# k's and q's features in one VectorE operation, inverse sums in PSUM, and the output pair's second half moved, in a two-block attention kernel

## The chip, the cores and the metric

The kernel runs on one NeuronCore of a Trainium2 chip. A core has five engines that run their own instruction queues in order and wait for each other through semaphores: TensorE (PE, matrix products), VectorE (DVE), ScalarE (ACT), GpSimd (POOL) and SyncE (SP, which only issues transfers here). Each has access to SBUF, the main on-chip memory; TensorE writes its results to PSUM, which has eight banks of 128 partitions x 512 fp32 values, and VectorE and ScalarE read them from there. The metric is the time of one execution on the device in microseconds (us). The kernel before takes 3023.89 us, the median of three runs (3023.61 to 3024.01).

## The reference

The input x is (8, 512, 64, 64): 8 images, 512 channels, 4096 positions. Two blocks follow each other, all in fp32.

The first block is softmax attention whose keys and values are max-pooled two by two, with 64 channels for f and g and 256 for v:

```python
f = conv1x1(x, Wf, bf).reshape(b, c // K, h * w)
g = maxpool2x2(conv1x1(x, Wg, bg))      # 1024 keys
v = maxpool2x2(conv1x1(x, Wh, bh))
s = jnp.einsum('bcn,bcm->bnm', f, g)
beta = jax.nn.softmax(s, axis=-1)
o = jnp.einsum('bcm,bnm->bcn', v, beta).reshape(b, c // 2, h, w)
x = gamma * conv1x1(o, Wv, bv) + x
```

The second is linear attention with 64 features for q and k:

```python
def delu(x):
    return PARAM * jax.nn.relu(x) + jnp.exp(PARAM * jnp.minimum(x, 0.0))   # PARAM = 10
Qf = delu(Q).transpose(0, 2, 1)
Kf = delu(K)
KV = jnp.einsum('bmn,bcn->bmc', Kf, V)
norm = 1.0 / jnp.einsum('bnd,bd->bn', Qf, jnp.sum(Kf, axis=-1) + EPS)
attn = jnp.einsum('bnd,bdc,bn->bcn', Qf, KV, norm)
out = x + gamma[0] * attn
```

KV and the sum of Kf need all positions of an image, so an image's second block can be finished only when its last position has been through the first.

## The kernel before, in words

An image is cut into 8 chunks of 512 positions, 64 chunks in all. The kernel is one software pipeline over steps s (function `step`); chunk s goes through the main part in step s. In the same step the projections of chunk s + 9 are made, so that pooled g and v of a whole image are ready before its first chunk is attended, and the image before is finished (`c_here`). Each step records its work as pairs of a number and a function, `at(t, fn, ...)`, sorts them by the number, and calls them in that order. The numbers are places in an order, not times that anything waits for. The engines PE, DVE, ACT and POOL keep the order written; only semaphores, and buffers that must come free, hold an instruction up.

In step s the work on TensorE stands in this order:

- M1 (line L433), the transposes of k of chunk s - 1 (`turn_k`, tile pkT, L581), M2, and the product of k and x of chunk s - 1 (`gather`, pg, L593), in even steps of an image to be finished pd (`normalize`, L673), then M3;
- the scores of chunk s + 1 (`weigh`, s, L347) between M6, M5, M7 and M4. M1 to M7 are the seven products of a Strassen-Winograd scheme for v times E (`attend`), E being the exponentials of the scores;
- in odd steps the first half of an output pair (`finish`, pa, L700): four matmuls of 512 columns from k's and v's product and q. A pair is two chunks whose q features share one tile (qq): one in the upper 64 partitions, the other in the lower;
- f and g of chunk s + 9 (`a_fg`, fg, L232), and tot (L390), the sums of E of chunk s + 1 over the keys, as a product with ones;
- N1 to N7 (`project`, L490), the output projection of chunk s as a Winograd scheme, H1 to H7 (`a_h`, L276), the projection to v of chunk s + 9;
- in odd steps the second half of the pair (pa again), the transposes of the pooled v (`a_turn`, pvT), k and q of chunk s (`features`, pk, L547), the transposes of x of chunk s (`turn_x`, px, L574). Then the next step's M1.

VectorE, in the same step: sums for M's outputs and E's sums r (L383, L386); the pooling of g (L209); `invert` (L395), the reciprocals of tot into an SBUF tile rtot; the N outputs (L506 to L523); `normalize_block` (L409), four multiplications of E of chunk s + 1 by rtot, with the H outputs (L285 to L299) in between; the pooling of v (vp, L209); the block sum T1 of E (`sums_of_e`, L415); the features kk (L560) and qq (L564), min(exp, 1) + relu, each for its half of the partitions; then T2, T3, T4 (L418 to L424). kk keeps k of one chunk in one half of the partitions and zeros in the other; its accumulator output goes to ks, from which `start_kb` (L616 to L623) sums k at the start of the next image and writes kb, the matrix of pd.

ScalarE makes the exponentials, copies from PSUM (m1, n1, h1, y, xT, kT), f's halves, x's bias, and `look` (L399, L400), which sums tot and its reciprocals into chk. After the pipeline chk is tested, and only if a sum was too large or small the whole is run again in another form. GpSimd makes some sums of E, the H inputs (tha, thb), adds the N outputs onto x (`residual`, L500), and issues the transfers that add y to the output in memory (L706). SyncE issues loads and the stores of x.

All PSUM tiles come from one pool of eight banks. A new tile takes a bank that is free in the written order, and its first matmul waits for the last reader of the tile that had the bank before. The pools named in the diff (f, q, y and others) work likewise in SBUF.

Of the kernel before, what the change touches and what calls it, by code (L numbers as in the profile page):

```python
# [42 lines left out]
P = 128  # L43
# [5 lines left out]
def tile_two_attention_blocks(  # L49
# [75 lines left out]
    nc.gpsimd.memset(ones, 1.0)  # L125

    kk = const.tile([P, CH], F32, name="kk")
    nc.gpsimd.memset(kk, 0.0)

    kb = const.tile([P, P], F32, name="kb")  # L130
    nc.gpsimd.memset(kb, 0.0)
# [29 lines left out]
    def half(e):  # L161
        return slice(e * D, (e + 1) * D)

    def run(ctx, general):
        xa = ctx.enter_context(tc.tile_pool(name="xa", bufs=2))
        xb = ctx.enter_context(tc.tile_pool(name="xb", bufs=2))
        yc = ctx.enter_context(tc.tile_pool(name="yc", bufs=1))
        image = ctx.enter_context(tc.tile_pool(name="image", bufs=2))
        fpool = ctx.enter_context(tc.tile_pool(name="fpool", bufs=10))
        qpool = ctx.enter_context(tc.tile_pool(name="qpool", bufs=6))  # L170
        work1 = ctx.enter_context(tc.tile_pool(name="work1", bufs=1))
        work = ctx.enter_context(tc.tile_pool(name="work", bufs=2))
        temp = ctx.enter_context(tc.tile_pool(name="temp", bufs=7))
# [41 lines left out]
        def image_of(a):  # L215
            b, j = divmod(a, NCHUNK)
            if j == 0 and b not in st:
                st[b] = {
                    "g": image.tile([P, MT // 2, P], F32, tag="g", name=f"g_{b}"),
                    "vT": image.tile([P, MT, CV], F32, tag="vT", name=f"vT_{b}"),  # L220
                    "ks": image.tile([P, NCHUNK // 2], F32, tag="ks", name=f"ks_{b}"),
                    "G": image.tile([P, C], F32, tag="G", name=f"G_{b}"),
                }
            return st[b]
# [166 lines left out]

        def invert(s):

            rtots[s] = work1.tile([P, CH], F32, tag="rtot", name=f"rtot_{s}")
            nc.vector.reciprocal(rtots[s], totals[s])  # L395

        def look(s):
# [75 lines left out]
        def project(s, at, t):  # L473

            m = {}

            def bias():
                for k in range(KT):
                    xs = x_b[s][:, k, :]
                    nc.scalar.activation(xs, xs, AF.Identity, bias=gb_v0[:, k : k + 1])  # L480

            def product(i):
                o, u = os_[s], to[s]
                b = {
                    1: o[:, 0, 0:HN], 2: o[:, 1, 0:HN], 3: o[:, 1, HN:CH],
                    4: u[:, 3], 5: u[:, 0], 6: u[:, 1], 7: u[:, 2],
                }[i]
                m[i] = bank(f"N{i}_{s}").rearrange("p (k n) -> p k n", k=2)
                for k in range(2):
                    nc.tensor.matmul(m[i][:, k, :], w_v7[i][:, bass.ts(k, P)], b, start=True, stop=True)  # L490
                if i == 1:
                    m["n1"] = part("n1")
                    nc.scalar.copy(m["n1"], m[1])

            def part(name):
                return scratch(f"{name}_{s}").rearrange("p (k n) -> p k n", k=2)

            def residual(i, j, u):
                d = x_b[s][:, 2 * i : 2 * i + 2, bass.ts(j, HN)]
                nc.gpsimd.tensor_tensor(d, d, u, ALU.add)  # L500

            def out(i):
                tt = nc.vector.tensor_tensor
                if i == 2:
                    u = part("n2")
                    tt(u, m["n1"], m[2], ALU.add)  # L506
                    residual(0, 0, u)
                elif i == 6:
                    m["u2"] = part("w2")
                    tt(m["u2"], m["n1"], m[6], ALU.add)  # L510
                elif i == 5:
                    u = part("n3")
                    tt(u, m["u2"], m[5], ALU.add)  # L513
                    tt(u, u, m[3], ALU.add)  # L514
                    residual(0, 1, u)
                elif i == 7:
                    m["u3"] = part("w3")
                    tt(m["u3"], m["u2"], m[7], ALU.add)
                    tt(m["u2"], m["u3"], m[5], ALU.add)
                    residual(1, 1, m["u2"])  # L520
                else:
                    u = part("n4")
                    tt(u, m["u3"], m[4], ALU.subtract)  # L523
                    residual(1, 0, u)

            def store():
                b, j = divmod(s, NCHUNK)
                nc.sync.dma_start(out=outr[b, :, :, bass.ts(j, CH)], in_=x_b[s])

            at(t - 7.4, bias)  # L530
            for n, i in enumerate((1, 2, 3, 6, 5, 7, 4)):
                at(t + 0.86 * n, product, i)
            for i, d in ((2, 3.4), (6, 4.1), (5, 4.8), (7, 6.2), (4, 7.6)):
                at(t + d, out, i)
            at(t + 10.0, store)

        def features(s, at, t):

            b, j = divmod(s, NCHUNK)
            e = j % 2  # L540
            k, q = half(e), half(1 - e)
            m = {}

            def product():
                pk = bank(f"pk_{s}")
                for i in range(KT):
                    nc.tensor.matmul(  # L547
                        pk, w_kqk[:, i, e * D : (e + 2) * D], x_b[s][:, i, :],
                        start=(i == 0), stop=(i == KT - 1),
                    )  # L550
                ex, r = m["ex"], m["r"] = scratch(f"e_{s}"), scratch(f"r_{s}")

                nc.scalar.activation(ex, pk, AF.Exp, bias=b10_kq[:, e : e + 1], scale=PARAM)
                nc.scalar.activation(r, pk, AF.Relu, bias=b10_kq[:, e : e + 1], scale=PARAM)

            def out():
                if e == 0:
                    qq[s // 2] = qpool.tile([P, CH], F32, tag="qq", name=f"qq_{s // 2}")
                ex, r = m["ex"], m["r"]
                nc.vector.scalar_tensor_tensor(  # L560
                    kk[k, :], ex[k, :], 1.0, r[k, :], ALU.min, ALU.add,
                    accum_out=st[b]["ks"][k, j // 2 : j // 2 + 1],
                )
                nc.vector.scalar_tensor_tensor(  # L564
                    qq[s // 2][q, :], ex[q, :], 1.0, r[q, :], ALU.min, ALU.add
                )

            at(t, product)
            at(t + 4.9, out)

        def turn_x(s, t):
            px = bank(f"px_{s}_{t}")
# [39 lines left out]
        def start_kb(b):  # L612

            s = st[b]
            kp = small.tile([P, 1], F32, tag="kp", name=f"kp_{b}")
            nc.vector.tensor_reduce(kp, s["ks"], AX.X, ALU.add)  # L616
            kx = small.tile([P, 1], F32, tag="kx", name=f"kx_{b}")
            nc.vector.tensor_copy(kx[0:D], kp[D : 2 * D])
            nc.vector.tensor_copy(kx[D : 2 * D], kp[0:D])
            ksum = s["ksum"] = image.tile([P, 1], F32, tag="ksum", name=f"ksum_{b}")  # L620
            nc.vector.tensor_tensor(ksum, kp, kx, ALU.add)
            for e in range(2):
                nc.vector.tensor_scalar(  # L623
                    kb[half(e), half(e)], ones[half(e), 0:D], ksum[half(e)], EPS, ALU.mult, ALU.add
                )
# [57 lines left out]
        def finish(pair, ks, at, t):  # L683
# [4 lines left out]
            def product():  # L688
                kv = st[b]["kv"]

                last = b == B - 1 and (2 * pair + ks[0] // 2) % 3 > 0
                pool_ = xa if last else yc
                y = m["y"] = pool_.tile(
                    [P, 2, 2, CH], F32, tag="xa" if last else "y", name=f"y_{pair}_{ks[0]}"
# [22 lines left out]
        def step(s):  # L717
# [24 lines left out]
                at(1.7, turn_k, s - 1)  # L742
                gather(s - 1, at, 3.9)
            if c_here and j == 0:
                at(1.8, start_kb, b_c)
                turn_G(b_c, at, 18.2 if here else 6.0)
                make_KV(b_c, at, 36.5 if here else 8.2)
            if c_here and here and j % 2 == 0:
                normalize(pair, at, 5.79)
            if c_here and not here and j == 0:  # L750
# [1 line left out]
                    normalize(pair + i, at, t)  # L752
            if c_here and j % 2 == 1:
                finish(pair, (0, 1), at, 18.2)
                finish(pair, (2, 3), at, 36.5)
            if 0 <= a < TOTAL:
                a_h(a, at, 20.7, 30.5, 40.8)
                a_fg(a, at, 20.0)
            if 0 <= a - 1 < TOTAL:
                at(5.0, bias_v, a - 1)  # L760
                at(38.3, a_turn, a - 1)
                if a % NCHUNK == 0:
                    at(39.0, sums_of_v, (a - 1) // NCHUNK)
            if after:
# [7 lines left out]
                at(15.9, lambda: add_next(n, nc.vector, "r1", es[n][:, 6, :]))  # L772
                at(17.3, lambda: add_next(n, nc.vector, "r1", es[n][:, 7, :]))
                at(18.1, lambda: add_next(n, nc.vector, "r1", sums[n, "r0"]))
                at(23.4, total, n)
                at(24.5, invert, n)
                if not general:
                    at(27.9, look, n)
                at(32.6, normalize_block, n, 0, 1)
                at(34.2, normalize_block, n, 0, 0)  # L780
                at(38.4, normalize_block, n, 1, 1)
                at(39.6, normalize_block, n, 1, 0)
                at(42.2, sums_of_e, n, 1)
            if here:
                project(s, at, 24.4)
                features(s, at, 38.6)
                for t in range(NT):
                    at(42.1 + t * 0.45, turn_x, s, t)
# [61 lines left out]
```

## Time and profile before

| | us | share of the span | instructions |
|---|---|---|---|
| span of the profiled execution | 3028.2 | | 32619 |
| PE, matmuls | 2871.4 | 95% | 11936 |
| DVE | 2411.3 | 80% | 3102 |
| ACT | 1110.7 | 37% | 2249 |
| POOL | 1132.2 | 37% | 809 |
| L409, E times rtot, 256 of them | 410.6 | | 1629 ns each |
| L395, the reciprocals of tot, 64 | 214.9 | | 3358 ns each |
| L560 and L564, kk and qq, 64 each | 49.5 and 48.7 | | 773 and 761 ns each |
| L703, copies of the output pair to y, 256 | 133.4 | | 600 ns each |

PE's time is that of matmuls; loads of weights (PEld) overlap them. A matmul record [...] may overlap the next: eight records of fg are 3.60 us in the timeline where each has a mean of 603 ns. The granted TensorE clock is a share of full speed, 0.982 in the mean over this run. In a list of waits each line gives the engine with the tile and line that waited, the one it waited for, and then microseconds in total, how often, and the longest. In a timeline a line gives start, duration, engine, line, operation, tiles and form, and in brackets the idle time of the engine ahead of it and who ended it.

The steps before 134 us fill the pipeline, those from 2957 us on empty it; from about 2620 us on there is no chunk s + 9 any more, so fg and H are gone.

### The profile page before, as it was taken

How to read it: one execution, taken by the hardware profiler on the slowest of the kernel's cores; microseconds unless marked ns; L12 is line 12 of the kernel's file. 1: busy time of each engine (PE TensorE's matmuls, PEld its weight loads, DVE VectorE, ACT ScalarE, POOL GpSimd, SP SyncE). 2: the span in 40 equal slices, each digit the busy share in tenths (PEclk: the TensorE clock that was granted, in tenths of full speed). 3: DMA queues.
4: the chain of work that ended last, by engine and by line, in shares of the span. 5: the costliest groups of instructions: out<-in, count | busy, mean ns of one | idle time of the engine just before them, and what ended most of it. 6: DMA issues, size and time to landing. Idle time of an engine off the chain costs nothing.

```text
span 3028.2 us, 32619 instructions
## 1 busy us (share of the span) xinstructions
PE 2871.4 (95%) x11936; PEld 1923.3 (64%) x11936; DVE 2411.3 (80%) x3102; ACT 1110.7 (37%) x2249; POOL 1132.2 (37%) x809
## 2 busy tenths in 40 slices
PE   8999999999999999999999999999999999999994
PEld 5666666666666666666666666666666666656662
DVE  4778878878788778888788788888788888788872
ACT  2333333333333333333433434333333433434432
POOL 4532434433443434333344333434325334232231
PEclk9999999999999999999999999999999999999997
DMA  5122212334234233333243333342233342233337
GB/s 179 51 75 84 70 56 84 98 84 111 75 93 112 74 108 91 91 98 111 70 121 89 82 99 99 97 111 84 74 108 96 99 112 56 70 98 84 84 84 154
DMA packets 128328, 280.98 MB, mean 93 GB/s; under 512 B 8480, under 2 KB 8992, under 8 KB 128160
## 3 DMA queue, kind: packets, MB, share of 16 engines
q1 hardware_dynamic: 105600, 209.73, 20.1%
q0 software_dynamic: 17408, 67.11, 12.6%
q10 hardware_dynamic: 5152, 1.97, 0.3%
q8 instruction: 97, 1.59, 0.2%
q14 instruction: 71, 0.58, 0.1%
HBM read 144.58 MB, written 134.22 MB: 92 GB/s over the span
## 4 chain that ended last, share of the span: by engine, by line
PE 55%; DVE 30%; issue 10%; ACT 3%; POOL 1%; DMA 0%; DVEq 0%; POOLq 0%; ACTq 0%
PE M L433 25%; DVE E L409 10%; PE s L347 8%; PE fg L232 7%; PE pg L593 4%; ACT f L250 3%; PE pa L700 2%; PE pk L547 2%; PE H L276 2%; DVE T L415 1%; DVE vp L209 1%; DVE n L513 1%; DVE n L514 1%; DVE n L506 1%; PE px L574 1%
## 5 line engine op out<-in xcount | busy, mean ns | idle before, releaser
L500 POOL TENSOR_TENSOR xb<-xb,n 128x512 f32<-128x512 f32 x192 | 306.2, 1595 | 560.7 <-DVE n L506 506.3
L351 ACT ACTIVATE E<-s 128x512 f32<-128x512 f32 x512 | 264.1, 603 | 634.0 <-PE s L347 628.7
L383 POOL TENSOR_TENSOR r<-E 128x512 f32<-128x512 f32 x64 | 81.0, 1266 | 983.0 <-ACT E L351 983.0
L409 DVE TENSOR_TENSOR E<-E,rtot 128x1024 f32<-128x1024 f32 x256 | 410.6, 1629 | 0.0
L433 PE MATMUL M<-T,S 128*128 128x256 f32 x1536 | 365.4, 388 | 0.0
L433 PEld LDWEIGHTS M<-T,S 128*128 128x128 f32 x1536 | 281.4, 190 | 128.7 <-ACT E L351 47.8
L433 PE MATMUL M<-E,vT 128*128 128x256 f32 x1024 | 268.3, 409 | 3.5 <-DVE E L409 3.5
L347 PE MATMUL s<-f,g 64*128 64x512 f32 x1024 | 254.1, 615 | 0.0
L232 PE MATMUL fg<-xa,w_fg 128*128 128x512 f32 x512 | 235.6, 603 | 12.3 <-DMA w_fg<-in_L_conv_Wg_dram 10.5
L547 PE MATMUL pk<-xb,w_kqk 128*128 128x512 f32 x512 | 233.3, 596 | 13.9 <-POOL xb L500 13.9
L490 PE MATMUL N<-to,w_v 128*128 128x256 f32 x1024 | 231.5, 379 | 0.0
L703 ACT COPY y<-pa 128x512 f32<-128x512 f32 x256 | 133.4, 600 | 244.3 <-PE pa L700 203.7
L433 PEld LDWEIGHTS M<-E,vT 128*128 128x128 f32 x1024 | 201.3, 207 | 29.9 <-issue 3.9
L395 DVE RECIPROCAL rtot<-tot 128x512 f32<-128x512 f32 x64 | 214.9, 3358 | 6.4 <-PE tot L390 4.6
L490 PEld LDWEIGHTS N<-to,w_v 128*128 128x128 f32 x1024 | 194.6, 190 | 26.5
L447 DVE TENSOR_TENSOR m<-m,M 128x256 f32<-128x256 f32 x64 | 26.9, 420 | 213.0 <-PE M L433 213.0
L276 PE MATMUL H<-xa,w_h 128*128 128x256 f32 x768 | 177.5, 381 | 0.0
L490 PE MATMUL N<-o,w_v 128*128 128x256 f32 x768 | 176.3, 379 | 0.0
L490 PEld LDWEIGHTS N<-o,w_v 128*128 128x128 f32 x768 | 145.8, 190 | 47.4 <-issue 29.9
L232 PEld LDWEIGHTS fg<-xa,w_fg 128*128 128x128 f32 x512 | 95.2, 192 | 125.7 <-issue 103.9
L386 POOL TENSOR_TENSOR r<-r,E 128x512 f32<-128x512 f32 x128 | 164.1, 1282 | 10.0
L700 PE MATMUL pa<-qq,kv 64*128 64x512 f32 x512 | 156.1, 629 | 10.1 <-ACT y L703 5.4
(127 smaller groups left out, 5180.0 us busy)
## 6 DMA issues: line engine op xcount, KB each, us to landing
xa<-in_x_dram SPq DMA_DIRECT2D x64, 1024.0 KB, 5.5
xb<-in_x_dram SPq DMA_DIRECT2D x64, 1024.0 KB, 5.5
out_dram<-xb SPq DMA_DIRECT2D x64, 1024.0 KB, 4.2
out_dram<-y POOLq DMA_DIRECT2D x64, 1024.0 KB, 8.3
w_v<-in_L_conv_wv_dram SPq DMA_DIRECT2D x8, 1024.0 KB, 5.4
w_h<-in_L_conv_Wh_dram ACTq DMA_DIRECT2D x1, 512.0 KB, 9.9
w_v<-in_L_conv_Wv_dram ACTq DMA_DIRECT2D x1, 512.0 KB, 6.4
w_kqk<-in_L_conv_wk_dram ACTq DMA_DIRECT2D x2, 128.0 KB, 7.7
```

Of the source, the lines that this page charges most:

```text
L232: nc.tensor.matmul(fg, w_fg[:, k, :], x_a[a][:, k, :], start=(k == 0), stop=(k == KT - 1))
L276: nc.tensor.matmul(m[i], w_h7[i][:, k, :], th[a][i][:, k, :], start=(k == 0), stop=(k == hk - 1))
L347: nc.tensor.matmul(sc[e], g[half(e), i, :], fs[s][half(e), :], start=True, stop=True)
L351: nc.scalar.activation(es[s][:, 2 * i + e, :], sc[e], AF.Exp)
L386: engine.tensor_tensor(sums[s, name], sums[s, name], e, ALU.add)
L395: nc.vector.reciprocal(rtots[s], totals[s])
L409: nc.vector.tensor_tensor(b, b, r, ALU.mult)
L433: nc.tensor.matmul(m[i], v7[i][:, k, :], te[s][i][:, k, :], start=(k == 0), stop=(k == hm - 1))
L490: nc.tensor.matmul(m[i][:, k, :], w_v7[i][:, bass.ts(k, P)], b, start=True, stop=True)
L500: nc.gpsimd.tensor_tensor(d, d, u, ALU.add)
L547: nc.tensor.matmul(pk, w_kqk[:, i, e * D : (e + 2) * D], x_b[s][:, i, :], start=(i == 0), stop=(i == KT - 1),)
L700: nc.tensor.matmul(pa, kv[hf, bass.ts(k, P)], qq[pair][hf, :], start=True, stop=True)
```

## The change

The parts, with the names of the functions above:

- `features`: kk and qq come from one operation over all 128 partitions into kk, whose accumulator output has a column per chunk in ks (8 in place of 4). ScalarE copies q's half from kk to qq. kk no longer keeps zeros, so its memset goes; the half that holds q (zeros before) is transposed along with k and not used. The operation is recorded at 43.3 (38.6 + 4.7), ahead of T1 (43.8) and of the pooling of v (43.9); before, it stood after both.
- `start_kb` sums the columns of even and of odd chunks apart, each for its half, and is moved from 1.8 to -1.0, ahead of the sums of E that a step starts with.
- `invert`: rtot is a PSUM bank in place of an SBUF tile, so L409 and `look` read it from there.
- `finish(pair, (2, 3))` moves from 36.5 to 23.5, behind f and g and ahead of tot. The first half stays at 18.2. The pool of y has two buffers in place of one, f's 9 in place of 10, and qq's 5 in place of 6. For the last image the second half of each pair uses x's buffers.
- the numbers of tot, the inversion, `project`, the multiplications, H and `make_KV` are raised by about 2, which makes room for the second half of the pair in the order.

The aim is that the transposes of k find kk ready, that VectorE has less to do, and that the second half of the pair no longer stands between H and k.

```diff
-    nc.gpsimd.memset(kk, 0.0)
...
-        yc = ctx.enter_context(tc.tile_pool(name="yc", bufs=1))
+        yc = ctx.enter_context(tc.tile_pool(name="yc", bufs=2))
-        fpool = ctx.enter_context(tc.tile_pool(name="fpool", bufs=10))
-        qpool = ctx.enter_context(tc.tile_pool(name="qpool", bufs=6))
+        fpool = ctx.enter_context(tc.tile_pool(name="fpool", bufs=9))
+        qpool = ctx.enter_context(tc.tile_pool(name="qpool", bufs=5))
...
-                    "ks": image.tile([P, NCHUNK // 2], F32, tag="ks", name=f"ks_{b}"),
+                    "ks": image.tile([P, NCHUNK], F32, tag="ks", name=f"ks_{b}"),
...
-            rtots[s] = work1.tile([P, CH], F32, tag="rtot", name=f"rtot_{s}")
+            rtots[s] = bank(f"rtot_{s}")
             nc.vector.reciprocal(rtots[s], totals[s])
...
-            at(t - 7.4, bias)
+            at(t - 9.3, bias)
...
                 nc.vector.scalar_tensor_tensor(
-                    kk[k, :], ex[k, :], 1.0, r[k, :], ALU.min, ALU.add,
-                    accum_out=st[b]["ks"][k, j // 2 : j // 2 + 1],
+                    kk, m["ex"], 1.0, m["r"], ALU.min, ALU.add, accum_out=st[b]["ks"][:, j : j + 1]
                 )
-                nc.vector.scalar_tensor_tensor(
-                    qq[s // 2][q, :], ex[q, :], 1.0, r[q, :], ALU.min, ALU.add
-                )
+                nc.scalar.copy(qq[s // 2][q, :], kk[q, :])
...
-            at(t + 4.9, out)
+            at(t + 4.7, out)
...
-            nc.vector.tensor_reduce(kp, s["ks"], AX.X, ALU.add)
+            ks = s["ks"].rearrange("p (j e) -> p e j", e=2)
+            for e in range(2):
+                nc.vector.tensor_reduce(kp[half(e)], ks[half(e), e, :], AX.X, ALU.add)
...
-                last = b == B - 1 and (2 * pair + ks[0] // 2) % 3 > 0
+                last = b == B - 1 and ks[0] > 0
...
-                at(1.8, start_kb, b_c)
+                at(-1.0, start_kb, b_c)
-                make_KV(b_c, at, 36.5 if here else 8.2)
+                make_KV(b_c, at, 38.5 if here else 8.2)
...
                 finish(pair, (0, 1), at, 18.2)
-                finish(pair, (2, 3), at, 36.5)
+                finish(pair, (2, 3), at, 23.5)
-                a_h(a, at, 20.7, 30.5, 40.8)
+                a_h(a, at, 20.7, 32.4, 43.9)
...
-                at(23.4, total, n)
-                at(24.5, invert, n)
+                at(25.3, total, n)
+                at(26.3, invert, n)
-                    at(27.9, look, n)
+                    at(29.8, look, n)
-                at(32.6, normalize_block, n, 0, 1)
-                at(34.2, normalize_block, n, 0, 0)
-                at(38.4, normalize_block, n, 1, 1)
-                at(39.6, normalize_block, n, 1, 0)
-                at(42.2, sums_of_e, n, 1)
+                at(34.5, normalize_block, n, 0, 1)
+                at(36.2, normalize_block, n, 0, 0)
+                at(40.3, normalize_block, n, 1, 1)
+                at(41.5, normalize_block, n, 1, 0)
+                at(43.8, sums_of_e, n, 1)
             if here:
-                project(s, at, 24.4)
+                project(s, at, 26.3)
```

## The prediction

> **What bounds the kernel now.** I read the page's busy line first, then who TensorE waited for, then one even step in order of time, and last the clock in two stretches. The busy line and one line of the costliest groups:
>
> ```profile
> span 3028.2 us, 32619 instructions
> PE 2871.4 (95%) x11936; PEld 1923.3 (64%) x11936; DVE 2411.3 (80%) x3102; ACT 1110.7 (37%) x2249; POOL 1132.2 (37%) x809
> L447 DVE TENSOR_TENSOR m<-m,M 128x256 f32<-128x256 f32 x64 | 26.9, 420 | 213.0 <-PE M L433 213.0
> ```
>
> TensorE is the bound: 157 us of the span are not matmul. VectorE once in a step stands idle for TensorE (213.0 us at L447, about 3.6 us each time), so it is in front there and has to be late somewhere else. The waits of TensorE (who, for whom, us in total, times, longest) say where:
>
> ```profile
> PE pkT L581 <- DVE kk L560: 72.3, 34, 3.9
> PE pk L547 <- POOL xb L500: 13.9, 11, 1.7
> ...
> PE pd L673 <- DVE kb L623: 4.7, 5, 0.9
> ...
> PE pa L700 <- DVE h L290: 4.0, 23, 0.2
> ```
>
> Half of the idle time is one wait: the transposes of k (pkT) wait for VectorE's kk. In order of time (start, us, engine, line) at the end of the even step s = 28, rows of three engines:
>
> ```profile
> 1425.73 1.98 DVE L409 TENSOR_TENSOR E<-E,rtot 128x1024 f32<-128x1024 f32 x1
> ...
> 1426.59 2.26 POOL L500 TENSOR_TENSOR xb<-xb,n 128x512 f32<-128x512 f32 x1
> ...
> 1432.27 2.35 DVE L409 TENSOR_TENSOR E<-E,rtot 128x1024 f32<-128x1024 f32 x2
> 1432.43 0.68 ACT L554 ACTIVATE r<-pk,b_kq 128x512 f32<-128x512 f32 x1
> ...
> 1433.39 1.89 PE L433 MATMUL M<-E,vT 128*128 128x256 f32 x8
> ...
> 1434.54 1.27 DVE L209 TENSOR_REDUCE vp<-h 128x128 f32<-128x512 f32 x2
> ...
> 1435.72 1.22 DVE L415 TENSOR_TENSOR T<-E 128x1024 f32<-128x1024 f32 x1
> 1436.86 0.68 DVE L560 SCALAR_TENSOR_TENSOR kk<-e,r 64x512 f32<-64x512 f32 x1
> ...
> 1437.60 0.66 PE L581 MATMUL pkT<-ident,kk 128*128 128x128 f32 x4 [2.32 <-DVE kk L560]
> ```
>
> M1 ends at 1435.28. The inputs of kk (e, r) are there at 1433.11, but VectorE first pools (1.27) and forms a block sum (1.22), both of which nobody needs for microseconds. Odd steps have no such wait: TensorE carries eight more matmuls (pa) there. Two even steps of the same work, as windows (length, PE, PEld, DVE, ACT, POOL busy, clock):
>
> ```profile
> 1411.61:1456.76 45.15, 42.83 (x185) 28.99 (x184) 37.00 (x51) 16.13 (x34) 17.36 (x12) 1.00 0.21 71
> 1501.68:1548.51 46.83, 44.51 (x185) 30.20 (x183) 36.95 (x49) 16.13 (x34) 17.91 (x13) 0.96 0.20 68
> ```
>
> Same 185 matmuls, 1.68 us more, and the clock is 0.96: behind the wait TensorE ran a stretch at half speed. The trace's clock record has 15 single stretches of 3.41 us and two double ones at 0.5, each within 1.5 us of the end of a pkT wait: 19 x 3.41 x 0.5 = 32.4 us. So this wait costs 72.3 + 32.4 = 104.7 us.
>
> [...] here a wait of 2.3 us is enough in about half of the cases. [...] L409 takes 1.98 and 1.96 us beside GpSimd's adds and 1.18 after them, an add takes 2.26 beside L409 and otherwise 1.27; VectorE's sums with a PSUM operand keep to 0.68 or 0.69 beside the same adds. [...] VectorE's gp does wait for ScalarE's f of the same bank (120.9 us in the waits).
>
> **The change part by part**, on s = 28.
>
> Features in one operation and ahead: kk for 128 partitions takes what it took for 64 (the median of both rows is about 0.69; upper bound 0.74 from the 128-partition L661), the 0.69 for qq is gone, and vp and T stand behind. From the second pair of L409 alone: 1434.62 + 0.68 + 0.08 (read of the accumulator) + 0.05 = 1435.43, 0.15 after M1. The wait falls from 2.32 to 0.15.
>
> Inverse sums in PSUM: the multiplication has one SBUF input left. Bounds: 1.22 [...] to 1.95 (as now). I take 1.22: 410.6 - 256 x 1.22 = 98 us off VectorE, 1.5 us of it per step ahead of kk. Then E ends at 1433.1, kk is held by r instead and ends near 1433.95, 1.3 us before M1 does. Wait: 0. That also holds in odd steps, where r is the later one: pk end + 1.47 + 0.8 against pk end + 3.5 for M1. The reciprocal's 3.36 us stays (bounds 3.3 and 3.5).
>
> What queues behind the earlier kk: T, vp, T2, T3, T4 now end about 6.1 after kk, 1.8 later than before relative to kk, kk being 1.3 ahead. T2 is needed by M6 8.5 us after pkT. Hidden by pg, M3 and the scores.
>
> New wait on ScalarE: the copy of q (0.60 to 0.74 by the rows of y and xb, I take 0.65) waits for kk, ahead of the last xT, m1 and kT. At kk = 1433.95: copy to 1434.6, xT to 1435.2, m1 after M1 at 1435.7, kT after pkT at 1436.4; TensorE needs kT only after M2, 1437.7. Hidden by M2. With kk at 1435.4 kT ends at 1437.3, still in time.
>
> One PSUM bank less from the inversion to the last multiplication. The order of the matmuls stays as it is except for pa and, at the start of an image, pkv; each H product now waits for one step later of the N outputs: H1 for n2, not the n1 copy. n2 ends at 1421.78, H1 starts at 1421.95: 0.17 left, at most 0.1 lost with the load of weights in front. In 40 steps that have no pa ahead of it: 0 to 4 us, I take 2. H2 to H4 have 0.4 to 1.9 us. [...]
>
> Second half of the pair behind f and g (odd steps): no work added. tot comes 1.9 us later, but VectorE works on gp and g until 1462.95 and tot would end at 1463.3: the inversion is 0.4 later, with over 3 us of room at pkT. ScalarE's four copies of y (2.05) run 1461.9 to 1464.0; the N products that take their banks start from 1464.1. GpSimd issues the store (1.2) at 1464 to 1465.2, its first add comes at 1467.4. The 0.17 us stop of pa (4.0 in all) goes. A second y buffer is needed for this and is there.
>
> The sums of k at the start of an image (start_kb) go ahead of T2: some 1.4 us of small operations earlier, so pd's 4.7 us go.
>
> One buffer less for f and for qq costs nothing: f of chunk n is made in step n-9 and last read in step n-1, so 8 live at once; of qq 5 live, and the sixth is made in the step after the oldest pair is finished. The memset of kk (0.5 us on GpSimd at the start) lies beside the first load.
>
> The last eight steps have no H, and pk waits for GpSimd's adds. Faster adds save 1.0 there; in odd steps tot 1.9 later costs it back: +0.9 and -1.0, together 0. The tail is eight stores, 5.0 us apart, at a DMA share of 1.06: unchanged.
>
> Sum: 72.3 less 2 that may stay, 32.4 clock, 4.7, 4.0, against 2 for H1: 3023.9 - 70.3 - 32.4 - 4.7 - 4.0 + 2 = 2914.5. Floor, with half of pk's 13.9 gone as well and nothing lost: 2904.
>
> **Rivals.** (1) A wait takes the place of the one removed. If H1 waits 0.5 us in 55 steps (VectorE late at n2), 27 us come back: 2942; if kT comes late because of the new copy, 0.5 us x 64 = 32 us: 2947. For it: 0.17 us of room at H1, three engines in one chain at kT. Against: both timelines above still fit at the slow bounds. (2) [...] the PSUM operand is slow itself: 0.15 us of wait stays in some 31 steps, 5 us, and a few half-clock stretches, say 4 x 1.7: 2926; it is within the forecast's range. (3) Slower: the second store now sits ahead of the adds in GpSimd's queue. If ScalarE's copies of y slip by 4 us behind other work, adds, pk, r and kk slip in all 32 odd steps, and each such gap brings 1.7 us of half clock: 32 x 5.7 = 182 - 112 = +70, 3094; with half of the slip about 3000. Against: 2.2 us of room between the issue and the first add.
>
> **How the numbers follow.** Forecast, including (2): 0.80. Rival (1): 0.13. No change, a half-sized (3): 0.02. Slower: 0.05. Predicted 2914. The range begins just under the floor at 2901 and goes to 2948, so that it takes in (1); about 0.1 lies above. Faster 0.93, same 0.02, slower 0.05.
>
> **What would show it.** TensorE's waits: pkT for kk under 5 us in all, no half-clock stretch between 140 and 2650 us, pd and pa gone from the list, H for n under 5 us. L409 with a mean near 1.22 us, GpSimd's L500 adds near 1.28, VectorE's busy time near 2270. All steps from s = 8 on with TensorE busy wall to wall. The prediction is wrong if pg waits for kT, if H1 waits for n2 in every step, or if the multiplications still take 1.95.

## The result, and the profile after

The changed kernel takes 2889.52 us (median of four runs, 2888.25 to 2890.22) beside 3023.95 for the kernel before (four runs, 3023.61 to 3028.35). The ratio is 0.9552, 95% interval 0.9535 to 0.9568: 134 us less. The forecast was 2914; its direction and its main cause held, and the time is 11 us under the low end of its range.

The busy line from the page of the changed kernel, then three of the costliest groups of its list (line, engine, operation, tiles and form, count | busy us in all, mean ns of one | idle time of the engine ahead of it, and who ended it).

```profile
span 2888.4 us, 32561 instructions
PE 2806.9 (97%) x11936; PEld 1899.9 (66%) x11936; DVE 2248.9 (78%) x3046; ACT 1141.2 (40%) x2313; POOL 1051.3 (36%) x808
...
L499 POOL TENSOR_TENSOR xb<-xb,n 128x512 f32<-128x512 f32 x192 | 244.9, 1276 | 433.1 <-DVE n L505 379.0 <-DVE n L513 54.0
...
L408 DVE TENSOR_TENSOR E<-E,rtot 128x1024 f32<-128x1024 f32 x256 | 304.3, 1215 | 1.6 <-ACT tot L399 1.6
L446 DVE TENSOR_TENSOR m<-m,M 128x256 f32<-128x256 f32 x64 | 26.9, 420 | 198.1 <-PE M L432 198.1
```

VectorE lost 162 us of work, 106 of them at the multiplications (410.6 to 304.3), and GpSimd 81. That saves nothing by itself, as neither is the bound. TensorE's idle time fell from 157 to 82 us. But its busy time fell too, by 64.5 us, for the same 11936 matmuls. That is the first thing to explain. Who TensorE waited for in the changed kernel (us in all, times, longest):

```profile
PE pk L546 <- POOL xb L499: 16.2, 16, 1.5
...
PE tot L389 <- DVE r L385: 6.5, 5, 4.0
...
PE pkT L576 <- DVE kp L613: 0.4, 1, 0.4
```

The wait of pkT for kk (72.3 before) is gone, and so are those of pd and of pa for h. What is left is pk's wait for GpSimd, mostly at the end, and single waits of the start and tail. The clock record has no stretch at half speed between 130 and 2700 us, where before had 64.8 us of them: 32.4 us of TensorE's busy time.

Of the other 32 us of busy time, 29 are the pair's second half. The group of pa, before and then after:

```profile
L700 PE MATMUL pa<-qq,kv 64*128 64x512 f32 x512 | 156.1, 629 | 10.1 <-ACT y L703 5.4 <-DVE h L290 4.0 <-DVE rn L677 0.7
```

```profile
L697 PE MATMUL pa<-qq,kv 64*128 64x512 f32 x512 | 127.1, 618 | 4.1 <-ACT y L700 3.4 <-DVE rn L674 0.7
```

512 matmuls in both, nearly the same mean (629 and 618 ns), but 29.0 us less time covered. The timeline shows why. First the second half of a pair in the kernel before, at the end of the odd step s = 29 (start, us, engine, line, tiles, count, and in brackets the idle time ahead and who ended it):

```profile
1473.15 1.96 DVE L409 TENSOR_TENSOR E<-E,rtot 128x1024 f32<-128x1024 f32 x1
...
1473.34 1.98 PE L700 MATMUL pa<-qq,kv 64*128 64x512 f32 x6
...
1475.03 0.41 DVE L290 TENSOR_TENSOR h<-h,H 128x256 f32<-128x256 f32 x1
1475.49 0.29 PEld L700 LDWEIGHTS pa<-qq,kv 64*128 64x128 f32 x2 [1.00 <-DVE h L290]
1475.49 1.12 PE L700 MATMUL pa<-qq,kv 64*128 64x512 f32 x2 [0.17 <-DVE h L290]
...
1475.99 0.42 DVE L292 TENSOR_TENSOR h<-h,H 128x256 f32<-128x256 f32 x1
...
1476.54 0.20 PEld L323 LDWEIGHTS pvT<-ident,vp 128*128 128x128 f32 x2 [0.76 <-DVE h L292]
```

And the same eight matmuls in their new place in the changed kernel:

```profile
1383.95 1.99 PE L697 MATMUL pa<-qq,kv 64*128 64x512 f32 x8
...
1385.87 1.12 PE L389 MATMUL tot<-r,ones 128*128 128x512 f32 x2
```

Read the starts, not the busy time. The group is four matmuls of 64 rows with two records each; two matmuls, one for each half of the partitions, run side by side: in the new place their first records start at 1383.950 and 1383.956. After, the eight records take 1385.87 - 1383.95 = 1.92 us to the next group. Before, they take 1476.54 - 1473.34 = 3.20. The starts of the single records in the trace say where, and they are the same in all 23 odd steps: the first six records come as in the new place, within 1.39 us, but the fourth matmul, the last two records, begins 2.16 us after the first record in place of 0.96. It waits for a bank that VectorE reads with L290, and L290 stands in VectorE's queue behind a multiplication of 1.96 us. So the third matmul runs alone (records from 1474.30 and 1474.73), and then the fourth (1475.49 and 1476.02). This costs 1.29 us in each of 23 odd steps, 29.7 in all. TensorE's matmul list has 0.17 us of it each time, 4.0 in all, because the third matmul keeps the engine busy while the fourth waits. The list of the weight loads of the kernel before has the wait, 1.00 us each time:

```profile
PEld pa L700 <- DVE h L290: 23.1, 23, 1.0
PEld pvT L323 <- DVE h L292: 17.4, 23, 0.8
PEld pa L700 <- DVE h L285: 7.6, 23, 0.3
```

The second line of it, pvT for L292, costs next to nothing: pvT starts 0.52 us after the last record of pa, as tot does in the new place.

The steps of the changed kernel, an even and an odd one as windows (length, PE, PEld, DVE, ACT, POOL busy with counts, clock, DMA share, GB/s):

```profile
1337.71:1380.32 42.61, 42.61 (x186) 28.99 (x184) 34.92 (x49) 16.72 (x35) 15.86 (x12) 1.00 0.22 75
1380.32:1424.00 43.68, 43.68 (x189) 29.67 (x187) 34.94 (x45) 18.67 (x39) 15.31 (x13) 1.00 0.50 121
```

TensorE is busy wall to wall at full clock; an even step took 45.15 before, or 46.83 with a half-clock stretch.

### The profile page after: what moved, and what is told of

Read it like the earlier page. It is cut to its first block, busy times and chain, and to the rows that moved or that the text cites. A ratio compares the mean times of both kernels' runs of the same rounds, so it can differ in the third digit from the quotient of the medians.

```text
span 2888.4 us, 32561 instructions
## 1 busy us (share of the span) xinstructions
PE 2806.9 (97%) x11936; PEld 1899.9 (66%) x11936; DVE 2248.9 (78%) x3046; ACT 1141.2 (40%) x2313; POOL 1051.3 (36%) x808
## 4 chain that ended last, share of the span: by engine, by line
PE 92%; issue 2%; DVE 2%; POOL 1%; DMA 1%; ACT 0%; ACTq 0%; POOLq 0%; DVEq 0%
PE M L432 28%; PE H L275 13%; PE N L489 12%; PE s L346 8%; PE fg L231 8%; PE pk L546 7%; PE pg L588 4%; PE px L569 4%; PE pa L697 4%; PE tot L389 2%; PE pd L670 1%; POOL xb L499 1%; PE pkT L576 1%; PE pkv L652 1%; DVE rtot L394 1%
## 5 line engine op out<-in xcount | busy, mean ns | idle before, releaser
L499 POOL TENSOR_TENSOR xb<-xb,n 128x512 f32<-128x512 f32 x192 | 244.9, 1276 | 433.1 <-DVE n L505 379.0
L408 DVE TENSOR_TENSOR E<-E,rtot 128x1024 f32<-128x1024 f32 x256 | 304.3, 1215 | 1.6 <-ACT tot L399 1.6
L546 PE MATMUL pk<-xb,w_kqk 128*128 128x512 f32 x512 | 233.3, 596 | 16.2 <-POOL xb L499 16.2
L432 PE MATMUL M<-E,vT 128*128 128x256 f32 x1024 | 243.6, 381 | 2.8 <-DVE E L408 2.8
L432 PEld LDWEIGHTS M<-E,vT 128*128 128x128 f32 x1024 | 185.2, 191 | 23.5 <-issue 3.2
L703 POOL DMA_DIRECT2D out_dram<-y x64 | 77.2, 1206 | 257.0 <-ACT y L700 255.9
L546 PEld LDWEIGHTS pk<-xb,w_kqk 128*128 128x128 f32 x512 | 92.1, 190 | 117.2 <-issue 90.9
```

Of the source, the lines that this page charges most:

```text
L408: nc.vector.tensor_tensor(b, b, r, ALU.mult)
L432: nc.tensor.matmul(m[i], v7[i][:, k, :], te[s][i][:, k, :], start=(k == 0), stop=(k == hm - 1))
L546: nc.tensor.matmul(pk, w_kqk[:, i, e * D : (e + 2) * D], x_b[s][:, i, :], start=(i == 0), stop=(i == KT - 1),)
```

## The experiments

Each run is compared by its ratio to the kernel before on the same chip. Before gave 3025.84, 3026.57, 3026.23 and 3027.21 us beside the four sets of runs (first, second, third, last). Beside the listed waits I use a distance between starts: from the first matmul of M1 to the first pkT. It is 1.73 us wherever kk is in time, in every kernel, and what goes beyond that is the true delay by kk. Summed over the steps it is 78.7 us in the kernel before (72.3 in the list) and 0.0 in the changed one.

**One part alone, on the kernel before** (the first set). The pair alone:

```diff
-        yc = ctx.enter_context(tc.tile_pool(name="yc", bufs=1))
-        fpool = ctx.enter_context(tc.tile_pool(name="fpool", bufs=10))
-        qpool = ctx.enter_context(tc.tile_pool(name="qpool", bufs=6))
+        yc = ctx.enter_context(tc.tile_pool(name="yc", bufs=2))
+        fpool = ctx.enter_context(tc.tile_pool(name="fpool", bufs=8))
+        qpool = ctx.enter_context(tc.tile_pool(name="qpool", bufs=5))
...
-                finish(pair, (2, 3), at, 36.5)
+                finish(pair, (2, 3), at, 23.42)
...
-                at(23.4, total, n)
+                at(23.44, total, n)
```

> The kernel before with one part of the change: the second half of the output pair behind f and g, ahead of tot (with two y buffers, and fewer of f and q to make room). My theory: in before, the second pa group after H takes 3.21 us where 1.92 would do, because its banks come free late, behind VectorE's slow multiplications of E; moved, it takes 1.92, 1.24 us less in each of 23 odd steps (-28). But tot and the inversion come 0.4 us later and the multiplications are still slow, so kk becomes late in odd steps too: about 0.8 us of new pkT wait in each, which gives back 19. Together 3013 us (3005 to 3020), with the even steps' 2.3 us waits as before. Rival, the stop is worth its full 28 us by itself: 2995. Rival, my recorded prediction (only 4 us there): 3020.

Measured: 3036.47 us, ratio 1.0034 (1.0021 to 1.0046), so 10.6 slower. TensorE's waits in this kernel:

```profile
PE pkT L581 <- DVE kk L560: 94.4, 52, 3.9
PE pk L547 <- POOL xb L500: 22.9, 17, 1.7
```

The stop is gone, 1.92 us in all 23 steps (29.7 won), and so is pd's wait for kb (4.7). But tot, and with it the whole queue of VectorE, comes later: kk is now late in odd steps too, by 0.94 us each (103.6 us of delay in place of 78.7), pk waits 9.0 more, 3.4 us go to half clock (71.7 us of stretches), and f, g and tot around the new place take 0.19 us more per odd step (4.4). Together -29.7 - 4.7 + 24.9 + 9.0 + 3.4 + 4.4 = +7.3, beside 6.2 between the two profiles (3034.4 and 3028.2) and 10.6 between the medians. I had foreseen the later kk and left out pk, half clock, f, g and tot.

k's and q's features in one operation ahead of T1 and pooling, alone:

```diff
-    nc.gpsimd.memset(kk, 0.0)
...
                 nc.vector.scalar_tensor_tensor(
-                    kk[k, :], ex[k, :], 1.0, r[k, :], ALU.min, ALU.add,
-                    accum_out=st[b]["ks"][k, j // 2 : j // 2 + 1],
-                )
-                nc.vector.scalar_tensor_tensor(
-                    qq[s // 2][q, :], ex[q, :], 1.0, r[q, :], ALU.min, ALU.add
+                    kk, m["ex"], 1.0, m["r"], ALU.min, ALU.add, accum_out=st[b]["ks"][:, j : j + 1]
                 )
...
-            at(t + 4.9, out)
+            at(t + 2.1, out)
+            at(t + 4.7, copy_q)
```

> The kernel before with the features in one VectorE operation ahead of the pooling and of T1, and q copied by ScalarE; inverse sums in SBUF, the pair where it was. My theory: even steps' wait falls from 2.32 to about 0.15 us (-67 to -70), the half-clock stretches behind it go (-32), the slow pa after H stays: 2923 us (2918 to 2932). Rival, the pkT wait needs the faster multiplications as well: half of the wait stays, 2970.

Measured: 2944.97, ratio 0.9735 (0.9719 to 0.9751). The delay by kk fell from 78.7 to 8.5 and half clock from 64.8 us of stretches to 3.4; start_kb, left in its old place, now makes pd wait (4.7 to 11.7):

```profile
PE pd L673 <- DVE kb L623: 11.7, 7, 2.0
...
PE pkT L579 <- DVE kk L558: 3.9, 2, 2.2
```

Those terms give -94; the profiled run, with a span of 2937.8 us, is 90 under the profile of before, the median 81. It is the fastest of the four runs and has a granted clock of 0.992, where the other three have 0.988 to 0.990, so half clock is the likely rest (an estimate from these clocks; the other runs have no trace). Fewer us than expected, part of it pd's. Is it the place or the merging? Only kk's own operation moved, the one for qq left where it was:

```diff
+            def out_q():
+                ex, r = m["ex"], m["r"]
                 nc.vector.scalar_tensor_tensor(
                     qq[s // 2][q, :], ex[q, :], 1.0, r[q, :], ALU.min, ALU.add
                 )
...
-            at(t + 4.9, out)
+            at(t + 2.1, out)
+            at(t + 4.9, out_q)
```

> The kernel before with nothing but the place of kk changed: its own 64-partition operation goes ahead of the pooling, qq's stays where it was. My theory: the place is all that counts for the wait, so the time is that of the one-operation version within 6 us: 2926 us (2920 to 2935). Rival, one operation less per step on VectorE (0.69 us) is what counts: 3000.

Measured: 2950.36, ratio 0.975 (0.9734 to 0.9766). Nearly all of it is the place: this interval overlaps that of the run before it. The merging is worth about the 5 us between the medians, within the noise. The profiles differ by 11 and put it in pd (15.7 for 11.7) and in half clock (17 us of stretches for 3.4).

The inverse sums in PSUM, alone:

```diff
-            rtots[s] = work1.tile([P, CH], F32, tag="rtot", name=f"rtot_{s}")
+            rtots[s] = bank(f"rtot_{s}")
```

> The kernel before with the inverse sums in a PSUM bank and nothing else. My theory: the multiplications of E go from 1.63 to 1.22 us in the mean, kk comes 1.5 us earlier, so the even steps' wait falls from 2.32 to about 0.8 (-46), and the second pa group, whose last bank waits for a VectorE sum behind two of the multiplications, loses about 1 us in 23 steps (-25). Half-clock stretches: if a gap of 0.8 us does not bring them, another -32: 2921; if it does as often as 2.3 us did, 2953. I expect 2930. Rival, [...] L409 stays at 1.63: 3024.

Measured: 2929.64, ratio 0.9682 (0.9666 to 0.9698). The multiplications in the groups, and then the wait, in this kernel:

```profile
L409 DVE TENSOR_TENSOR E<-E,rtot 128x1024 f32<-128x1024 f32 x256 | 304.3, 1214 | 1.6 <-ACT tot L400 1.6
```

```profile
PE pkT L581 <- DVE kk L560: 21.7, 27, 0.9
```

The multiplications are as fast as in the changed kernel, with nothing else changed, so the PSUM operand is what does it. kk comes 1.5 us sooner. In most even steps it is still 0.96 late, 25.5 us in all, and not one of these gaps brought a half-clock stretch. One line of code brings 96 us, the largest part by itself: 53.2 at pkT by the starts, 32.4 of half clock, 10.6 at pa (2.75 us a group), and 8.0 at pk and pd make 104, beside 101 between the profiles. That the forecast of 2930 was met is in part luck: it had 46 at pkT and 25 at pa, and half clock somewhere between gone and not.

**One part taken out of the changed kernel** (the second set, with the third and last). The second half of the pair back behind H:

```diff
-                finish(pair, (2, 3), at, 23.5)
+                finish(pair, (2, 3), at, 38.0)
```

> The changed kernel with the second half of the pair put back between H and the transposes of v. Theory A (the pa stop came from banks held behind the slow multiplications, and fast ones clear it): pa takes about 2.1 us there, 5 us lost in 23 steps, and about 8 us won after the last H because tot comes earlier in odd steps: 2887 (2880 to 2896). Theory B (standing behind H costs 1.24 us in itself): 2889.5 + 28 = 2918, less the 8.

Measured: 2897.37, ratio 0.9572 (0.9556 to 0.9588), between the two theories. As this interval touches that of the changed kernel, both were run again on one chip, the changed kernel unaltered:

> The changed kernel itself, unaltered, as the yardstick for the other two on the same chip: 2889.5, ratio 0.955.

> The changed kernel with the second half of the pair behind H again, beside the unaltered one on the same chip. If its earlier place is worth the 19 us of stop less 9 us of waits of pk: 6 to 10 us slower than the unaltered one. Rival (the earlier 8 us were a difference of chips): within 2 us of it.

Measured: 2887.67 unaltered, ratio 0.9541 (0.9528 to 0.9555), and 2898.62 with the pair behind H, 0.9577 (0.9564 to 0.9591). So the place is worth 11 us here. The weight loads of the second of these:

```profile
PEld pvT L322 <- ACT y L700: 17.4, 23, 0.8
PEld pa L697 <- DVE h L291: 12.4, 23, 0.5
PEld pa L697 <- DVE h L289: 9.5, 23, 0.4
```

The group takes 2.75 us from start to start: 0.83 us of stop in 23 steps, 19.1 in all, against 29.7 in the kernel before. The fast multiplications clear a third of the stop, the new place the rest. Its price is at pk, whose wait is 16.2 with the new place and 7.0 without. -19.1 + 9.2 = -9.9, beside 11.0 measured.

The sums back in SBUF:

```diff
-        fpool = ctx.enter_context(tc.tile_pool(name="fpool", bufs=9))
+        fpool = ctx.enter_context(tc.tile_pool(name="fpool", bufs=8))
...
-            rtots[s] = bank(f"rtot_{s}")
+            rtots[s] = work1.tile([P, CH], F32, tag="rtot", name=f"rtot_{s}")
```

> The changed kernel with the inverse sums back in SBUF. Theory: the multiplications take 1.63 us in the mean again; even steps wait 0.15 us for kk (about 5 us with the first eight steps), GpSimd's last add is slow again in the last eight steps (8 us): 2903 (2896 to 2910). Rival, the PSUM part carries half of the whole gain: 2950 or more.

One buffer of f was given up to make room for rtot. Measured: 2914.9, ratio 0.9628 (0.9612 to 0.9644): 25 us slower than the changed kernel by the medians, 23 by the ratios (27 and 26 beside the unaltered kernel run again). The multiplications take 1644 ns again, and the even steps inside an image show a delay of 0.15 or 0.16 us at pkT, which is the figure the prediction worked out for multiplications that stay slow. With delays of up to 2.3 us at the edges of images it makes 15.2 us; pk adds 6.7 and half clock 1.7: 23.6.

The features as before, two operations behind T1 and pooling, without the copy on ScalarE:

```diff
                 nc.vector.scalar_tensor_tensor(
-                    kk, m["ex"], 1.0, m["r"], ALU.min, ALU.add, accum_out=st[b]["ks"][:, j : j + 1]
+                    kk[k, :], ex[k, :], 1.0, r[k, :], ALU.min, ALU.add,
+                    accum_out=st[b]["ks"][k, j : j + 1],
+                )
+                nc.vector.scalar_tensor_tensor(
+                    qq[s // 2][q, :], ex[q, :], 1.0, r[q, :], ALU.min, ALU.add
                 )
-                nc.scalar.copy(qq[s // 2][q, :], kk[q, :])
...
-            at(t + 4.7, out)
+            at(t + 5.4, out)
```

> The changed kernel with k's and q's features as two operations again, behind T1 and the pooling of v as before, and without the copy on ScalarE; sums in PSUM and the pair's place stay. Theory A (the fast multiplications bring VectorE 1.5 us forward per step, but the old order asks for 2.5 us, and the earlier pair makes tot and with it kk 0.4 us later in odd steps): a wait of pkT of 0.8 to 1.3 us in most of the 64 steps, 40 to 60 us in all, no half-clock stretch: 2930 to 2950. Rival B (with the sums in PSUM the order of the features hardly matters): under 10 us of wait, 2890 to 2900.

Measured: 2919.65, ratio 0.9645 (0.9631 to 0.9659), on the same chip 32.0 above the unaltered kernel. TensorE's wait for kk in this kernel:

```profile
PE pkT L581 <- DVE kk L560: 24.2, 32, 1.7
```

The delay between starts is 28.9 us: 0.96 in most even steps and, against theory A, none in the odd steps inside an image, where 1.5 us from the multiplications cover the 0.94 that the pair's new place costs. Rival B is wrong by more: the order still counts. Theory A had the wait too long (40 to 60 us) and the time 10 us too high. No stretch at half clock follows these waits; the one at 2700 us follows a wait of pk.

`start_kb` back in its place, the third set:

```diff
-                at(-1.0, start_kb, b_c)
+                at(1.8, start_kb, b_c)
```

> The changed kernel with the sums of k for kb recorded at 1.8 again, so behind T2 and T3 on VectorE instead of ahead of T2. Theory: with kk ahead of T1 and of the pooling, kb comes about 6.3 us after kk, some 1 to 2 us too late for pd at the start of each of the 7 images finished in the pipeline (as pd's wait of 11.7 us in the features-only kernel suggests): 10 us in all, 2900 (2894 to 2906). Rival: kk's new head start hides it and only pd's old 4.7 us or less return: 2892.

Measured: 2897.73, ratio 0.9572 (0.9556 to 0.9588). The wait that comes back is one line in the list of this kernel:

```profile
PE pd L670 <- DVE kb L620: 8.4, 7, 1.3
```

8.4 us by the list and 8.2 between the medians, on chips whose kernels before differ by 2.3; beside the unaltered kernel that was run again on the same chip it is 10.1. The wait is certain, the exact worth is not.

**Where else the pair could stand.** In the kernel before, behind k and q, where the banks it takes have long been read:

```diff
-                finish(pair, (2, 3), at, 36.5)
+                finish(pair, (2, 3), at, 38.7)
```

> The kernel before with the second half of the pair 3.7 us later, behind pk instead of ahead of pvT and pk; nothing else. By then VectorE has read all the H banks that pa takes over. Theory (banks): pa takes 1.92 us instead of 3.21, and about 0.4 us comes back as a pkT wait in odd steps: -0.9 in 23 steps, 3003 (2996 to 3012). Rival (pa is slow behind H for another reason, as the loads of its weights): 3024, pa still above 3.

Measured: 3006.98, ratio 0.9934 (0.9917 to 0.995), the second set. The stop vanishes here too, with the group of pa at the same pace as in the new place, so it came from the banks next to H. The delay by kk grows by 10.1 and pk's wait by 9.0, while half clock loses 15.4. That the time met the forecast was luck: the forecast had neither pk's wait nor the half clock.

**A faster version.** The new place costs at pk only in the last eight steps, which have no f and g, and the list of the changed kernel has a wait of 7.7 us before the tail's first pkv. So there:

```diff
-                for i, t in enumerate((5.79, 5.8, 12.0, 12.1)):
+                for i, t in enumerate((6.3, 12.0, 12.1, 12.2)):
                     normalize(pair + i, at, t)
...
-                finish(pair, (2, 3), at, 23.5)
+                finish(pair, (2, 3), at, 23.5 if a < TOTAL else 38.0)
```

> The changed kernel with two moves in its end: from the step where f, g and H are gone on, the second half of the pair goes behind the N products again, so that tot does not wait for it (odd steps' pk wait from about 2.1 to 0.2 us, -8); and after the last chunk the first inversion for q is recorded behind G's transposes' sums, so that the sums for k's and v's product do not wait for two of them (the first store 6.5 us earlier, -6.5). Expected 2875 us (2870 to 2882). Rival: the stores at the end are bound by the transfers alone and the odd steps by something else: 2889.

Measured: 2872.29 (2871.84 to 2872.83), ratio 0.9489 (0.9473 to 0.9504), faster than both kernels. Its list of waits:

```profile
PE pk L546 <- POOL xb L499: 6.9, 9, 1.5
...
PE pkv L652 <- PE pd L670: 0.7, 1, 0.7
```

9.3 and 7.0 us came off where they were meant to: 16.3 of the 17.2 between the medians.

The parts together, in us of the median:

| part | added alone to the kernel before | taken out of the changed kernel |
|---|---|---|
| features ahead and in one | -81 | +32 |
| sums in PSUM | -96 | +25 to +27 |
| pair's second half | +11 | +11 |
| start_kb ahead | not run alone | +8 to +10 |

Two parts remove the same wait: either one takes most of it, so what they bring alone doesn't add up. The pair is the reverse. Alone it loses, as it makes kk later where kk was already late; once kk has room, the same edit wins.

## Where the prediction was right, and which step was wrong

- **pkT's wait for kk**: 72.3 less 2 that may stay. Measured 0.4 (and that for kp, at the start). By the starts 78.7 went, 6 more than the list showed.
- **Half clock**: 32.4 us, all gone. Right. A wait brings it "in about half of the cases": what the trace shows of which ones stands in the last section.
- **Multiplications in PSUM**: 1.22 us taken, 1.215 measured; a sum of that size in SBUF (L415) has a mean of 1.233 in the profile before. GpSimd's adds 1.276 (1.28 said), the reciprocal 3.366 (3.36 kept). That one SBUF input less would bring the full 1.22 was the author's estimate, and it held: 1629 to 1215 ns in the whole change and 1214 for that line alone, which also takes GpSimd's adds from 1595 to 1273.
- **H1 waiting for n2**: 2 us taken, 0 measured; no wait of H for n is in the list. The 0.17 us of room was enough.
- **Copy of q on ScalarE**: 0.65 taken, 0.622 measured. pg's wait for kT is one of 1.2 us in all. Hidden, as worked out.
- **pd**: 4.7 gone. Right; without the move of start_kb it would have been 8.4.
- **Last eight steps**: "together 0". pk's wait went from 13.9 to 16.2, so 2.3 lost.
- **The rivals** (a wait at H1 or kT, GpSimd's queue) did not happen. Rival 2's figure of 0.15 us of remaining wait is what the kernel with SBUF sums shows.

**The step that failed** is the one on the second half of the pair: "The 0.17 us stop of pa (4.0 in all) goes." The mechanism is right, the stop goes, but its size was off: 1.29 us per odd step and 29.7 in all, in place of 0.17 and 4.0. I read TensorE's matmul waits as all the time that it loses. But a matmul that should run beside another and comes late leaves no idle time in the list as long as the other one runs: in step s = 29 the third matmul of the group starts alone at 1474.30 and its second record at 1474.73, and the fourth, due beside it at 1474.30, comes at 1475.49, 1.19 late, of which the list keeps 0.17. The lengths of the records don't show it either: the one from 1474.73 is 0.59 us long, where the next start of the group in its new place comes 0.43 to 0.53 later. The lateness is plain in the weight loads and in the starts. I had the start of each step in the windows, and an odd step of 44.92 beside what its matmuls should take would have shown it.

With 29.7 for 4.0 the prediction's sum is 2914.5 - 25.7 = 2888.8; measured 2889.5. So close a hit is luck in part, as other terms were off and cancel. Between the two profiles, 3028.2 - 2888.4 = 139.8 us, the sum closes: 78.7 at pkT, 32.4 of half clock, 29.7 at pa and 4.7 at pd are 145.5; pk loses 2.3, and the first M1 comes 2.8 us later in the profile after (159.25 for 156.49), which is not the edit's doing, as it comes at 155.61 in the second profile of the same kernel. That leaves 140.4. The 0.19 us more at f, g and tot in odd steps come back as shorter groups of H, pvT and pkT (0.20 in step s = 29).

But the medians are only 134.4 apart: the profiled execution of the kernel before took 3029.98 us, 6 above the median of 3023.9. The prediction took the terms of that slower execution off the median, 6 too much. Its list was 6.4 short at pkT, and of the 2 at H1 and the 2 that might stay at pkT nearly nothing came, which hid it. What the slower execution spent its 6 us on isn't recorded; of the thirty-one runs of the kernel before beside the experiments, those at 0.981 or 0.982 of the full clock are mostly the longer ones (up to 3033.72 us) and those at 0.984 mostly the shorter ones (from 3022.85), and this one had 0.982.

The floor of 2904 was no floor, since it was built on the list of waits.

## What to carry to other kernels

Before an edit to TensorE's order is costed, compare start to start with the same group where it runs freely, and read the weight loads' waits; a busy matmul row can hide more than a microsecond of bank wait per group (1.29 us here, where 0.17 stood in the list), above all where two matmuls should run side by side. An operand in PSUM is worth a bank if it frees VectorE and GpSimd from each other, as it did here (1629 to 1214 ns for a multiplication, 1595 to 1273 for an add), ahead of something that TensorE waits for. Edits that make the same queue earlier don't add up, and an edit that makes it later can lose alone and win behind them, so cost them in the order in which they are made.

## What the runs showed of the hardware beyond what was expected

- TensorE went to half clock without a whole idle stretch of 3.4 us. In the traces of the kernel before and of the changed kernel the changes of the granted clock lie whole multiples of 3.413 us apart. I added up the matmul records in each window of that length, cut at those places, between 140 and 2650 us that itself ran at full clock. In the kernel before they cover 23% to 39% of 16 windows, and each time the next window ran at half speed; of the other 701 they cover 43% or more, and it never did. In the changed kernel they cover 57% or more of all 734, and none was followed by half speed.
- So here the place of a gap counted along with its length. Of the 25 delays of about 2.5 us in the kernel before, 15 brought one stretch (the window from 1524.54 us is covered to 32%) and 10 none (that from 1435.80 to 47%). The two of 3.7 and 4.1 us brought two stretches each. Delays of 0.96 to 1.09 us, with only the PSUM edit or with the features put back, leave 73% or more and brought none; five of 1.4 us and one of 1.9 in the kernel with SBUF sums brought none, one of 2.3 did. Near the end, where other matmuls run, one window with 45% brought a stretch (2697 us, features put back), so these shares are what was measured for one mix of matmuls.
- A multiplication of 128x1024 fp32 values with one operand in PSUM, read with a repeat, takes the same 1.215 us as an undisturbed sum of that size in SBUF (1.22). The reciprocal from bank to bank takes 3.366 us, into SBUF 3.358.
- Four matmuls over 64 of the 128 rows (eight records), two side by side with starts 6 or 7 ns apart, take 1.92 us from start to start, while each record has a mean of 618 ns. The fourth of a group takes 1.05 us to the next group where it runs alone in the kernel before, about as long as a pair.
